# A denoising layer and a 5x5 layer on one core: cosine products on 32x32 tiles, products moved within VectorE's order, transfers written in smaller pieces

## The chip, the core and the metric

The kernel runs on one core of a Trainium2 chip, in float32 throughout. The core has TensorE (PE in the profile; its weight loads are PEld), VectorE (DVE), ScalarE (ACT), GpSimd (POOL) and SyncE (SP). POOL and SP here mostly issue transfers, which 16 DMA engines carry out. The metric is the device time of one execution in microseconds.

## The reference

The input x has 8 images of 32 channels and 128 x 128 pixels. Layer 0 normalises x in groups of two channels, finds for each pixel the 8 of 25 neighbouring offsets with the least patch distance, and gathers the 8 shifted copies into 256 channels (xb). On these it computes

```
dct    = conv1x1(xb, dct_w, groups=32)           # 8x8 blocks, one per input channel
h      = relu(depthwise3x3(conv1x1(xb, w1), w2))
h      = relu(depthwise3x3(conv1x1(h, w3), w4))
wiener = sigmoid(depthwise3x3(conv1x1(h, w5), w6))
x      = x + conv1x1(conv1x1(wiener * dct, inv_dct_w, groups=32), agg_w)
```

Layer 1 normalises the new x in the same groups, convolves every channel with one 5 x 5 kernel, and adds the result to x.

## The kernel before

**Steps.** An image is worked through in strips of 8 rows (R), 16 strips and one more step for the rows that lag behind, so 17 steps an image and 136 in all, in one loop over `s`. In each pass of the loop there are four slots, i = 3, 2, 1, 0. Slots 1 to 3 are the three blocks of a 1x1 convolution and a depthwise one, each on another strip (strip s in slot 1, s-1 in slot 2, s-2 in slot 3); slot 0 finishes the strip of slot 3: it forms the cosine transform and multiplies the sigmoid's output with it. Beside that, each slot gathers one quarter of the strip that the next pass needs: `gather_load` (L584) loads the indices as ib and the pixels as xt, `gather_select` (L610) makes one-hot rows (sel) on ScalarE, `gather_pixels` (L620) multiplies them on TensorE (pg) and copies the outcome into xb, which is stored in device memory as xbd (L640).

**The two halves of a block.** The 256 channels are two halves of 128. For one, `pointwise_t` (L680) and `depthwise_t` (L733) do both convolutions on TensorE (p at L694, pw at L751). For the other, `pointwise_v` (L659) uses TensorE (pv at L670), and `depthwise_v` (L711) does one product on ScalarE (L722) and eight multiply-adds on VectorE (L725), then the activation (L729). `depthwise_v` is a generator: the multiply-adds are written out in the slot of its block, the activation in the next slot (as `dv`), and the transfer of the two rows for the next strip in the one after it (as `kept`).

**The cosine transform.** `final_load` (L770) loads the strip's x (xr) and its 256 gathered channels (xf, one buffer) at the end of slot 0, one pass ahead of their use. `final_dct` (L796) multiplies xf with ldct on 64x64 tiles of TensorE into pc (L810), four rows at a time, each PSUM tile filled by two row groups of the array, and VectorE multiplies the blocks' output by pc in place (L818, here "the products"). `final_add` (L820) multiplies the products with lagg (pa, L831) in the next pass's slot 3; then VectorE adds xr (L839), takes statistics (L840), and four transfers store x1d (L844). ldct is made once by `mixes` (L300) from 32 small loads of dct_w on SP (dq, L308).

**PSUM.** The pool `ps_x` has five tiles of 512 columns, which pv, p, pg, pc, pa, layer 1's products and several transposes share.

**What sets the order.** The loop is written out by hand for TensorE, VectorE and ScalarE: what stands first in the code is first in the engine's order. POOL's and SP's instructions are not in that list; the framework's scheduler places their transfers, so they need not follow the code. Work for the next image (`prep`, `squares`, `costs`, `places`, `sources`) and layer 1 of the image before (`layer1`, `middle`) is cut into tasks in queues: B and D hold VectorE work with costs and due times, which `tick` spends by credit in each slot; A, P and Q hold work that is run whole at fixed places of the slot (P before `final_dct`, Q after it, A near the end). A task that yields a queue's name goes on when that queue is next run, and not before the stated number of ticks. `sources` (L399) ends in one row of some 30 transfers from POOL (xtd, L424), once an image; `costs` (L485) issues 13 (dsum, L492 and L499).

Of the kernel before, what the change touches and what calls it, by code (L numbers as in the profile page):

```python
# [20 lines left out]
R = 8  # L21
# [23 lines left out]
def bm3d_conv_preact(  # L45
# [61 lines left out]
    ldct = const.tile([P, 2, 64], F32, name="ldct")  # L107
# [96 lines left out]
    queues = {"B": deque(), "D": deque(), "A": deque(), "P": deque(), "Q": deque()}  # L204
# [95 lines left out]
    def mixes():  # L300

        dq = work.tile([P, 2, K], F32, name="dq", tag="dq", bufs=1)
        src = dct_w.rearrange("(m h c i) k a b -> m h k c (i a b)", m=2, h=2, i=K)
        for k in range(K):
            for m in range(2):
                for h in range(2):
                    p = 64 * h + 32 * (k % 2) + 8 * (k // 2)
                    nc.sync.dma_start(dq[p : p + 8, m], src[m, (h + m + 1) % 2, k])  # L308
        m8 = work.tile([P, 8], F32, name="m8", tag="m16", bufs=1)
        yield "D", 1.0, 10  # L310
        nc.vector.tensor_reduce(
            m8,
            cst[:, C_M32 : C_M32 + C].rearrange("p (a c) -> p c a", c=8),
# [3 lines left out]
        for m in range(2):  # L317
            nc.vector.tensor_tensor(
                ldct[:, m].rearrange("p (c i) -> p c i", i=K),
                m8.unsqueeze(2).to_broadcast([P, 8, K]),  # L320
                dq[:, m].unsqueeze(1).to_broadcast([P, 8, K]),
                ALU.mult,
            )
# [296 lines left out]
    def gather_pixels(b, s4, f):  # L620

        n, h = s4 // 2, s4 % 2
        if h == 0 and f == 0:
            xbs[b, n] = xbp.tile([P, 2, R, W], F32, name=f"xb_{b}_{n}", tag="xb")
        xb, xt = xbs[b, n], xts[b, s4]
        sels = [selss.pop((b, s4, f, k2)) for k2 in range(2)]
        pg = ps_x.tile([P, 2, 4, HW], F32, name=f"pg_{b}_{s4}_{f}", tag="x")
        for t in range(NT // 2):
            xa, xz = TW * t, min(TW * (t + 1), HW)
            for j in range(4):  # L630
                nc.tensor.matmul(  # L631
                    pg[C * j : C * (j + 1), :, :, xa:xz],
                    xt[: 8 * QW, f * (NT // 2) + t],
                    sels[j // 2][: 8 * QW, j % 2 * 2 : j % 2 * 2 + 2, :, xa:xz],
                    start=True,
                    stop=True,
                )
        nc.scalar.copy(xb[:, :, 4 * h : 4 * h + 4, HW * f : HW * (f + 1)], pg)
        if h == 1 and f == 1:
            nc.gpsimd.dma_start(xbd[b][:, :, R * n : R * (n + 1)], xb)  # L640
# [70 lines left out]
    def depthwise_v(i, b, n):  # L711
# [4 lines left out]
        for k, (dy, dx) in enumerate(  # L716
# [7 lines left out]
            else:  # L724
                nc.vector.scalar_tensor_tensor(  # L725
# [44 lines left out]
    def final_load(b, n):  # L770
# [15 lines left out]
        src = xbd[b].rearrange("(j m h c) g y x -> g m h j c y x", j=4, m=2, h=2)  # L786
        for m in range(2):
            for h in range(2):
                for g in range(2):
                    p = 64 * h + C * g  # L790
                    nc.gpsimd.dma_start(  # L791
                        xf[p : p + C, m, j0:j1], src[g, m, (h + m + 1) % 2, :, :, ya:yz]
                    )
        return xr, xf, j0, j1

    def final_dct(b, n, acc, xf, j0, j1):  # L796

        for r0 in range(0, R, 4):
            a, z = max(r0, j0), min(r0 + 4, j1)
            if a >= z:  # L800
                continue


            pc = [
                ps_x.tile([P, 4, W], F32, name=f"pc_{b}_{n}_{m}_{r0}", tag="x") for m in range(2)
            ]
            for h in range(2):
                for m in range(2):
                    o = 64 * ((h + m + 1) % 2)
                    nc.tensor.matmul(  # L810
                        pc[m][o : o + 64, : z - a],
                        ldct[64 * h : 64 * h + 64, m],
                        xf[64 * h : 64 * h + 64, m, a:z],
                        start=True,
                        stop=True,
                    )
            for m in range(2):
                nc.vector.tensor_mul(acc[m][:, a:z], acc[m][:, a:z], pc[m][:, : z - a])  # L818

    def final_add(b, n, acc, xr, j0, j1):  # L820
# [19 lines left out]
        nc.vector.bn_stats(stats[b][:, n], xr)  # L840
        for j in range(4):
# [6 lines left out]
    def layer1(b):  # L848
# [60 lines left out]
        for c in range(0, C, 8):  # L909
# [3 lines left out]
            yield "P", 0  # L913
# [20 lines left out]
            for e in range(2):  # L934
                y = t[2 * e]
                nc.vector.tensor_add(y, y, ps[e])
                for a, z in ((0, 62), (66, P)):
                    nc.gpsimd.dma_start(
                        out[b, c + 4 * e : c + 4 * e + 4, a:z].rearrange("c y x -> y c x"),
                        y[a:z],  # L940
# [83 lines left out]
    def turn(credit):  # L1024
# [4 lines left out]
        run("P")  # L1029
        run("Q")  # L1030
# [5 lines left out]
    with tc.manual_schedule(engines=ORDERED):  # L1036
# [3 lines left out]
        xbd[0] = dram.tile([P, 2, H, W], F32, name="xbd_0", tag="xbd")  # L1040
# [15 lines left out]
        for s in range(len(steps) + 2):  # L1056
            if s < len(steps):
# [6 lines left out]
                if n == NS - 1 and b + 1 < NB:  # L1064
                    until(lambda: b + 1 in ready, 4.0)
                    xbd[b + 1] = dram.tile([P, 2, H, W], F32, name=f"xbd_{b+1}", tag="xbd")
            for i in (3, 2, 1, 0):
# [6 lines left out]
                if live and i:  # L1074
# [3 lines left out]
                    accs[i, bi, ni] = [None, next(new_v)]  # L1078
                next(later, None)
# [6 lines left out]
                if live and not i:  # L1086
                    final_dct(bi, ni, accs[3, bi, ni], xf, j0, j1)

# [14 lines left out]
                next(dv, None)  # L1103
# [3 lines left out]
                next(dt, None)  # L1107
                kept, dv, dt = dv, new_v, new_t
                if live and not i:
                    later = end(bi, ni, xr, j0, j1)  # L1110
                if not i and 0 <= s - 1 < len(steps):
                    fins[s - 1] = final_load(*steps[s - 1])
# [66 lines left out]
```

## Time and profile before

| | |
|---|---|
| median of 3 runs | 6535.1 us (6530.16 to 6537.6) |
| the profiled execution | 6526.97 us |
| its span | 6525.2 us |
| granted TensorE clock, mean | 0.979 of full speed |
| PE, DVE, ACT, POOL busy | 95%, 90%, 77%, 47% of the span |
| transfers | 886.21 MB in 544960 packets, 136 GB/s |
| first and last pc (L810) | 287.9 and 6459 us |

A group of the profile names the line, the engine, the operation, and the tiles as out<-in, with how often it occurs, its busy time, the mean of one, and the idle time of its engine just before it with what ended that idle time. A line of waits reads: the engine and the tile that waited, what it waited for, the sum of the waits in us, how many, and the longest. In a line of the timeline stand start and length in us, and instructions of one kind in a row are put together, their number behind x. A float32 matmul of the code is two records.

### The profile page before, as it was taken

To read this page: it belongs to the slowest core of one execution; us is meant where nothing else is said; L and a number is where in the kernel's file an instruction comes from. 1 tells how busy PE (TensorE), PEld (TensorE's weight loads), DVE (VectorE), ACT (ScalarE), POOL (GpSimd) and SP (SyncE) were. 2 spreads that over 40 slices of the span, in tenths; PEclk is the share of its full clock that TensorE was granted. 3 is DMA by queue.
4 is the path that set the end of the run, shared out by engine and by line. 5 is a ranking of instruction groups with operands and counts; after the bars stand their busy time and mean duration, and the time that the engine had idled before them with its cause. 6 is when DMAs were issued, how large, how long until landed. Compare 5 with 4: busy or idle time off the path is not lost.

```text
span 6525.2 us, 234180 instructions
## 1 busy us (share of the span) xinstructions
PE 6180.3 (95%) x102306; PEld 3262.3 (50%) x102306; DVE 5856.5 (90%) x8828; ACT 5051.0 (77%) x6698; POOL 3077.3 (47%) x5015
## 2 busy tenths in 40 slices
PE   5799999999999999999999999999999999999997
PEld 1445445544555546454555544544545454465553
DVE  7899988999889998899998999899998999988776
ACT  5787769778787877877778787887869787787772
POOL 8345436444364444643446534454345644344334
PEclk7899999999999999999999999999999999999998
DMA  4555555565555655655546556565555665455553
GB/s 85 125 135 144 123 124 146 145 143 135 133 145 139 142 147 127 150 140 135 141 129 157 140 131 151 127 150 137 139 134 138 150 147 133 118 149 147 137 135 79
DMA packets 544960, 886.21 MB, mean 136 GB/s; under 512 B 248880, under 2 KB 312944, under 8 KB 543936
## 3 DMA queue, kind: packets, MB, share of 16 engines
q0 software_dynamic: 383648, 611.87, 37.4%
q1 hardware_dynamic: 157776, 258.11, 16.4%
q8 instruction: 805, 13.19, 0.9%
q10 hardware_dynamic: 2512, 1.25, 0.1%
q14 instruction: 219, 1.79, 0.1%
HBM read 420.60 MB, written 216.49 MB: 98 GB/s over the span
## 4 chain that ended last, share of the span: by engine, by line
PE 50%; DVE 32%; ACT 5%; POOL 5%; DMA 4%; issue 4%; SPq 0%; ACTq 0%; DVEq 0%; POOLq 0%
DVE acc L725 21%; PE pw L751 16%; PE pv L670 12%; PE p L694 11%; PE pg L631 4%; DVE idx L537 3%; POOL xtd L424 3%; PE pc L810 2%; DVE df L444 2%; DVE acc L818 1%; PE p L924 1%; DVE mx L536 1%; PE pd L459 1%; DMA t<-t 1%; ACT sel L616 1%
## 5 line engine op out<-in xcount | busy, mean ns | idle before, releaser
L725 DVE SCALAR_TENSOR_TENSOR acc<-tv,dwv,acc 128x1024 f32<-128x1024 f32 (+3 forms) x3264 | 4031.6, 1237 | 156.3 <-ACT acc L722 52.0
L751 PE MATMUL pw<-t,dwd 96*32 96x254 f32 (+7 forms) x31680 | 2118.1, 419 | 23.0 <-DMA t<-t 10.1
L751 PEld LDWEIGHTS pw<-t,dwd 96*32 96x32 f32 (+1 forms) x31680 | 1105.7, 110 | 826.8 <-issue 369.3
L616 ACT ACTIVATE sel<-ib,nplace 128x1024 f32<-128x1024 uint8 x1024 | 1170.8, 1143 | 62.0 <-DMA ib<-idxd 62.0
L617 ACT ACTIVATE sel<-sel 128x1024 f32<-128x1024 f32 x1024 | 1086.0, 1061 | 32.5
L670 PE MATMUL pv<-acc,lw 128*32 128x512 f32 x8448 | 959.8, 590 | 54.4 <-DVE acc L818 47.8
L694 PE MATMUL p<-acc,lw 128*32 128x256 f32 x16768 | 974.3, 379 | 2.2 <-issue 2.2
L602 POOL DMA_DIRECT2D ib<-idxd x512 | 292.0, 570 | 1207.3 <-ACT sel L616 1078.1
L791 POOL DMA_DIRECT2D xf<-xbd x1088 | 651.0, 632 | 279.9 <-PE pc L810 180.6
L694 PEld LDWEIGHTS p<-acc,lw 128*32 128x32 f32 x16768 | 570.7, 111 | 393.6 <-issue 67.4
L729 ACT ACTIVATE acc<-acc 128x1024 f32<-128x1024 f32 (+3 forms) x408 | 417.1, 1022 | 390.2 <-DVE acc L725 389.8
L678 ACT COPY tv<-pv 128x512 f32<-128x512 f32 (+2 forms) x784 | 435.9, 579 | 338.5 <-PE pv L670 334.1
L631 PE MATMUL pg<-sel,xt 120*32 120x88 f32 (+1 forms) x24576 | 611.7, 244 | 64.8 <-ACT sel L617 56.1
L631 PEld LDWEIGHTS pg<-sel,xt 120*32 120x32 f32 x24576 | 559.5, 111 | 219.2 <-ACT sel L617 74.4
L670 PEld LDWEIGHTS pv<-acc,lw 128*32 128x32 f32 x8448 | 290.2, 110 | 532.3 <-issue 409.7
L764 ACT ACTIVATE acc<-pw 128x512 f32<-128x512 f32 (+2 forms) x808 | 436.6, 572 | 133.4 <-PE pw L751 131.8
L444 DVE TENSOR_TENSOR df<-xn 128x786 f32<-128x786 f32 (+2 forms) x576 | 530.4, 972 | 2.2 <-PE pd L459 1.9
L701 ACT COPY t<-p 128x512 f32<-128x512 f32 x800 | 421.7, 571 | 115.4 <-PE p L694 115.4
L452 ACT ACTIVATE df<-df 128x786 f32<-128x786 f32 (+2 forms) x576 | 458.9, 859 | 50.0 <-DVE df L444 48.6
L722 ACT ACTIVATE acc<-tv,dwv 128x1024 f32<-128x1024 f32 (+3 forms) x408 | 455.1, 1115 | 42.3 <-PE pa L831 24.8
L670 PE MATMUL pv<-xb,lw 128*32 128x512 f32 x4096 | 470.8, 596 | 0.0
L694 PE MATMUL p<-xb,lw 128*32 128x256 f32 x8192 | 469.9, 380 | 0.0
(155 smaller groups left out, 5893.0 us busy)
## 6 DMA issues: line engine op xcount, KB each, us to landing
ib<-idxd POOLq DMA_DIRECT2D x512, 256.0 KB, 4.0
xbd<-xb POOLq DMA_DIRECT2D x128, 1024.0 KB, 6.0
xf<-xbd POOLq DMA_DIRECT2D x960, 128.0 KB, 6.8
t<-t SPq DMA_DIRECT2D x792, 128.0 KB
t<-t SPq DMA_DIRECT2D x384, 256.0 KB
tv<-tv SPq DMA_DIRECT2D x384, 130.0 KB
xt<-xtd POOLq DMA_DIRECT2D x240, 180.0 KB, 4.0
xtd<-xl POOLq DMA_DIRECT2D x192, 96.0 KB, 3.3
```

What stands on the lines that cost most here:

```text
L444: nc.vector.tensor_sub(df[:, :, ca:cz], xn[:, r0 : r0 + SR, ca:cz], xn[:, r0 + dy : r0 + dy + SR, ca + dx : cz + dx],)
L452: nc.scalar.activation(df[:, :, ca:cz], df[:, :, ca:cz], AF.Square)
L616: nc.scalar.activation(sel, ib, AF.Square, bias=nplace)
L617: nc.scalar.activation(sel, sel, AF.Relu, scale=-1.0, bias=1.0)
L631: nc.tensor.matmul(pg[C * j : C * (j + 1), :, :, xa:xz], xt[: 8 * QW, f * (NT // 2) + t], sels[j // 2][: 8 * QW, j % 2 * 2 : j % 2 * 2 + 2 ...
L670: nc.tensor.matmul(ps[C * j : C * (j + 1), :hr], lhsT[:, g, P + C * j : P + C * (j + 1)], src(g)[:, h : h + hr], start=g == 0, stop=g == 1,)
L694: nc.tensor.matmul(ps[C * r : C * (r + 1), e, :nb], lhsT[:, g, s], rows[:, r : r + 4 * nb - 3 : 4], start=g == 0, stop=g == 1,)
L722: nc.scalar.activation(acc, rows, AF.Copy, scale=tap)
L725: nc.vector.scalar_tensor_tensor(acc, rows, tap, acc, op0=ALU.mult, op1=ALU.add)
L751: nc.tensor.matmul(pt[u][C * j : C * (j + 1), ka:kz, :nb, xa:xz], dwd[0:hi, i - 1, u, j, dx + 1], t[0:hi, j, ka:kz, :nb, xa + dx : xz + dx ...
L764: nc.scalar.activation(rows[:, u : u + 2 * nh[u] - 1 : 2, :nb], pt[u][:, : nh[u], :nb], funcs[i - 1])
L791: nc.gpsimd.dma_start(xf[p : p + C, m, j0:j1], src[g, m, (h + m + 1) % 2, :, :, ya:yz])
```

## The change

The cosine transform goes from 64x64 to 32x32 tiles. ldct holds four 32 x 32 blocks per partition group rather than two of 64 columns, made from 64 small loads rather than 32. In `final_dct`, s counts four parts (two halves of the channels times two groups of four rows), each with its own PSUM tile, and q four row groups of the array; part s takes from row group q to column group (q + s) % 4, so that each PSUM tile is filled by all four row groups. All 16 matmuls of a strip now come before the first product.

xbd is laid out by channel. A strip is stored in two times four transfers, after each four rows, rather than in one. xf is loaded part by part, up to seven transfers in place of eight: the first part at the end of slot 0, the second at the end of the next pass's slot 3, the last two at the end of its slot 2.

In the first block, `depthwise_v` stops after six of its eight multiply-adds; the last two are written out in slot 0 behind `final_dct`, and its activation moves to the next pass's slot 3.

The four x1d transfers of `final_add` and the four output transfers of `layer1` are written some way behind the VectorE instructions that make their data. Layer 1's matmuls get a queue of their own, L, which is run in place of `final_dct` where a slot has none.

```diff
--- before.py
+++ after.py
@@ -104,7 +104,7 @@
     lw5 = const.tile([P, 2, CK], F32, name="lw5")
 
 
-    ldct = const.tile([P, 2, 64], F32, name="ldct")
+    ldct = const.tile([P, 4, C], F32, name="ldct")
     lagg = const.tile([P, 2, C], F32, name="lagg")
 
 
@@ -201,7 +201,7 @@
 
 
 
-    queues = {"B": deque(), "D": deque(), "A": deque(), "P": deque(), "Q": deque()}
+    queues = {"B": deque(), "D": deque(), "A": deque(), "P": deque(), "L": deque(), "Q": deque()}
 
     PAIR = 1.95
     pairs = [0]
@@ -299,26 +299,26 @@
 
     def mixes():
 
-        dq = work.tile([P, 2, K], F32, name="dq", tag="dq", bufs=1)
-        src = dct_w.rearrange("(m h c i) k a b -> m h k c (i a b)", m=2, h=2, i=K)
-        for k in range(K):
-            for m in range(2):
-                for h in range(2):
-                    p = 64 * h + 32 * (k % 2) + 8 * (k // 2)
-                    nc.sync.dma_start(dq[p : p + 8, m], src[m, (h + m + 1) % 2, k])
-        m8 = work.tile([P, 8], F32, name="m8", tag="m16", bufs=1)
+        dq = work.tile([P, 4, K], F32, name="dq", tag="dq", bufs=1)
+        src = dct_w.rearrange("(m q c i) k a b -> m q c k (i a b)", m=2, q=4, i=K)
+        for s in range(4):
+            for q in range(4):
+                for c in range(4):
+                    p = C * q + K * c
+                    nc.sync.dma_start(dq[p : p + K, s], src[s // 2, (q + s) % 4, c])
+        m4 = work.tile([P, 4], F32, name="m4", tag="m16", bufs=1)
         yield "D", 1.0, 10
         nc.vector.tensor_reduce(
-            m8,
-            cst[:, C_M32 : C_M32 + C].rearrange("p (a c) -> p c a", c=8),
+            m4,
+            cst[:, C_M32 : C_M32 + C].rearrange("p (a c) -> p a c", a=4),
             axis=mybir.AxisListType.X,
             op=ALU.add,
         )
-        for m in range(2):
+        for s in range(4):
             nc.vector.tensor_tensor(
-                ldct[:, m].rearrange("p (c i) -> p c i", i=K),
-                m8.unsqueeze(2).to_broadcast([P, 8, K]),
-                dq[:, m].unsqueeze(1).to_broadcast([P, 8, K]),
+                ldct[:, s].rearrange("p (c i) -> p c i", i=K),
+                m4.unsqueeze(2).to_broadcast([P, 4, K]),
+                dq[:, s].unsqueeze(1).to_broadcast([P, 4, K]),
                 ALU.mult,
             )
 
@@ -636,8 +636,14 @@
                     stop=True,
                 )
         nc.scalar.copy(xb[:, :, 4 * h : 4 * h + 4, HW * f : HW * (f + 1)], pg)
-        if h == 1 and f == 1:
-            nc.gpsimd.dma_start(xbd[b][:, :, R * n : R * (n + 1)], xb)
+        if f == 1:
+            for j in range(4):
+                nc.gpsimd.dma_start(
+                    xbd[b].rearrange("(c j g) y x -> j c g y x", j=4, g=2)[
+                        j, :, :, 4 * s4 : 4 * s4 + 4
+                    ],
+                    xb[C * j : C * (j + 1), :, 4 * h : 4 * h + 4],
+                )
 
 
 
@@ -722,6 +728,8 @@
                 nc.scalar.activation(acc, rows, AF.Copy, scale=tap)
                 yield out_
             else:
+                if i == 1 and k == 7:
+                    yield
                 nc.vector.scalar_tensor_tensor(
                     acc, rows, tap, acc, op0=ALU.mult, op1=ALU.add
                 )
@@ -783,39 +791,41 @@
             )
 
         xf = xbp.tile([P, 2, R, W], F32, name=f"xf_{b}_{n}", tag="xf", bufs=1)
-        src = xbd[b].rearrange("(j m h c) g y x -> g m h j c y x", j=4, m=2, h=2)
-        for m in range(2):
-            for h in range(2):
-                for g in range(2):
-                    p = 64 * h + C * g
+        yield xr, xf, j0, j1
+        src = xbd[b].rearrange("(m p) y x -> m p y x", m=2)
+        for s in range(4):
+            if s:
+                yield
+            m, r0 = s // 2, s % 2 * 4
+            a, z = max(r0, j0), min(r0 + 4, j1)
+            for pa, pz, at in ((0, P - C * s, C * s), (P - C * s, P, 0)):
+                if a < z and pa < pz:
                     nc.gpsimd.dma_start(
-                        xf[p : p + C, m, j0:j1], src[g, m, (h + m + 1) % 2, :, :, ya:yz]
+                        xf[pa:pz, m, a:z],
+                        src[m, at : at + pz - pa, R * n - 3 + a : R * n - 3 + z],
                     )
-        return xr, xf, j0, j1
+        yield
 
     def final_dct(b, n, acc, xf, j0, j1):
 
-        for r0 in range(0, R, 4):
-            a, z = max(r0, j0), min(r0 + 4, j1)
-            if a >= z:
-                continue
-
-
-            pc = [
-                ps_x.tile([P, 4, W], F32, name=f"pc_{b}_{n}_{m}_{r0}", tag="x") for m in range(2)
-            ]
-            for h in range(2):
-                for m in range(2):
-                    o = 64 * ((h + m + 1) % 2)
-                    nc.tensor.matmul(
-                        pc[m][o : o + 64, : z - a],
-                        ldct[64 * h : 64 * h + 64, m],
-                        xf[64 * h : 64 * h + 64, m, a:z],
-                        start=True,
-                        stop=True,
-                    )
-            for m in range(2):
-                nc.vector.tensor_mul(acc[m][:, a:z], acc[m][:, a:z], pc[m][:, : z - a])
+        parts = [(s, max(s % 2 * 4, j0), min(s % 2 * 4 + 4, j1)) for s in range(4)]
+        parts = [(s, a, z) for s, a, z in parts if a < z]
+        pc = {
+            s: ps_x.tile([P, 4, W], F32, name=f"pc_{b}_{n}_{s}", tag="x") for s, a, z in parts
+        }
+        for q in range(4):
+            for s, a, z in parts:
+                o = C * ((q + s) % 4)
+                nc.tensor.matmul(
+                    pc[s][o : o + C, : z - a],
+                    ldct[C * q : C * (q + 1), s],
+                    xf[C * q : C * (q + 1), s // 2, a:z],
+                    start=True,
+                    stop=True,
+                )
+        for s, a, z in parts:
+            m = s // 2
+            nc.vector.tensor_mul(acc[m][:, a:z], acc[m][:, a:z], pc[s][:, : z - a])
 
     def final_add(b, n, acc, xr, j0, j1):
 
@@ -838,6 +848,7 @@
         yield
         nc.vector.tensor_add(xr, xr, pa)
         nc.vector.bn_stats(stats[b][:, n], xr)
+        yield
         for j in range(4):
             ra = ya + 2 * j if whole else ya
             xa = 0 if whole else C * j
@@ -910,7 +921,7 @@
             if c == 0 or not last:
                 yield "D", 2.0, 1 if last else 3
                 normalise(c)
-            yield "P", 0
+            yield "L", 0
             ps = [
                 ps_x.tile([P, 4, W], F32, name=f"p5_{b}_{c}_{e}", tag="x") for e in range(2)
             ]
@@ -932,12 +943,13 @@
             if last and c + 8 < C:
                 normalise(c + 8)
             for e in range(2):
-                y = t[2 * e]
-                nc.vector.tensor_add(y, y, ps[e])
+                nc.vector.tensor_add(t[2 * e], t[2 * e], ps[e])
+            yield "A", 0, 1
+            for e in range(2):
                 for a, z in ((0, 62), (66, P)):
                     nc.gpsimd.dma_start(
                         out[b, c + 4 * e : c + 4 * e + 4, a:z].rearrange("c y x -> y c x"),
-                        y[a:z],
+                        t[2 * e][a:z],
                     )
             if c + 8 < C and not last:
                 yield "A", 0, 1
@@ -1027,6 +1039,7 @@
         run("B")
         run("A")
         run("P")
+        run("L")
         run("Q")
 
     def until(cond, credit):
@@ -1037,7 +1050,7 @@
         push(prep(0))
         push(weights())
         push(mixes())
-        xbd[0] = dram.tile([P, 2, H, W], F32, name="xbd_0", tag="xbd")
+        xbd[0] = dram.tile([CK, H, W], F32, name="xbd_0", tag="xbd")
         for i in range(3):
             nc.gpsimd.memset(tb[i][0:64, 0], 0.0)
         for u in range(7):
@@ -1076,6 +1089,8 @@
                     pointwise_v(i, bi, ni, lws[i - 1], src)
                     new_v, new_t = depthwise_v(i, bi, ni), depthwise_t(i, bi, ni)
                     accs[i, bi, ni] = [None, next(new_v)]
+                if i == 3:
+                    next(kept, None)
                 next(later, None)
                 if live and not i:
                     if ni == 0:
@@ -1085,6 +1100,10 @@
                 run("P")
                 if live and not i:
                     final_dct(bi, ni, accs[3, bi, ni], xf, j0, j1)
+                else:
+                    run("L")
+                if not i:
+                    next(dv, None)
 
                 run("Q")
                 if s < len(steps):
@@ -1100,16 +1119,22 @@
                     unit(gather_pixels, u)
                 next(dt, None)
                 run("A")
-                next(dv, None)
+                if i:
+                    next(dv, None)
                 if s < len(steps):
                     unit(gather_select, u + 1, (1,))
                     u += 1
                 next(dt, None)
+                next(later, None)
                 kept, dv, dt = dv, new_v, new_t
                 if live and not i:
                     later = end(bi, ni, xr, j0, j1)
                 if not i and 0 <= s - 1 < len(steps):
-                    fins[s - 1] = final_load(*steps[s - 1])
+                    loads = final_load(*steps[s - 1])
+                    fins[s - 1] = next(loads)
+                if 0 <= s - (1 if not i else 2) < len(steps):
+                    for _ in range({0: 1, 3: 1, 2: 2, 1: 0}[i]):
+                        next(loads)
         next(kept, None)
         for _ in later:
             pass
...
```

The hunk left out changes the shape of xbd[b + 1] like that of xbd[0].

More of the change, by code (lines that the diff above doesn't have):

```diff
@@ L1065, in bm3d_conv_preact @@
                     until(lambda: b + 1 in ready, 4.0)
[L1066 removed]
+                    xbd[b + 1] = dram.tile([CK, H, W], F32, name=f"xbd_{b+1}", tag="xbd")
             for i in (3, 2, 1, 0):
```

## The prediction

> **What bounds the kernel now.** First the busy times and the 40 slices of the page.
>
> ```profile
> PE 6180.3 (95%) x102306; PEld 3262.3 (50%) x102306; DVE 5856.5 (90%) x8828; ACT 5051.0 (77%) x6698; POOL 3077.3 (47%) x5015
> PE   5799999999999999999999999999999999999997
> DVE  7899988999889998899998999899998999988776
> ```
>
> PE is full from the third slice on, DVE nearly so. Then the stretch from the first cosine product (pc, L810) to the last, and two single steps in it, each from one step's pc to the next.
>
> ```profile
> 287.90:6459.00 6171.10, 5972.12 (x100058) 3171.29 (x100054) 5600.56 (x8145) 4869.65 (x6449) 2867.30 (x4719) 0.99 0.55 138
> 2836.20:2885.30 49.10, 49.10 (x820) 24.37 (x820) 46.61 (x81) 41.20 (x53) 19.85 (x34) 1.00 0.61 152
> 3032.00:3080.60 48.60, 45.40 (x778) 23.10 (x774) 47.09 (x80) 37.63 (x50) 13.11 (x24) 1.00 0.49 121
> ```
>
> The columns are window, length, then busy time of PE, PEld, DVE, ACT and POOL. Over the stretch PE is idle for 199 us of 6171. In the step at 2836 PE has no gap at all. In the step at 3032 PE is idle for 3.2 us, while DVE misses only 1.5 us over 80 instructions, about 20 ns each, which is no more than the seam between two instructions: that step is DVE's. So two engines take turns as the bound, step by step. Whatever PE saves counts only in PE's steps.
>
> Last the waits between these two.
>
> ```profile
> PE pv L670 <- DVE acc L818: 47.8, 28, 3.6
> DVE xr L839 <- PE pa L831: 261.2, 69, 9.8
> ```
>
> PE waits 47.8 us for the products (L818), which hold four of the five PSUM tiles that pv needs; DVE waits 261 us for pa.
>
> **Part 1: the cosine product on 32x32 tiles.**
>
> ```profile
> 3308.16 1.95 PE L810 MATMUL pc<-xf,ldct 64*64 64x512 f32 x16
> 3310.04 5.37 PE L751 MATMUL pw<-t,dwd 96*32 96x256 f32 x96
> 3315.22 3.62 PE L670 MATMUL pv<-acc,lw 128*32 128x512 f32 x32
> 3318.66 1.04 PE L831 MATMUL pa<-acc,lagg 128*32 128x256 f32 x16
> 3322.97 1.14 PE L631 MATMUL pg<-sel,xt 120*32 120x88 f32 x48
> 3323.92 3.63 PE L670 MATMUL pv<-acc,lw 128*32 128x512 f32 x32
> ```
>
> A matmul of the code is two records (8 in the code, x16 here). From start to next start pc takes 1.88 us per whole step: 16 records of 512 columns on four tiles, so 0.47 us for four at once. pv, also four tiles, takes 3.44/32 x 4 = 0.43 us. The new form has 16 matmuls, 32 records of 512 columns, for 16 tiles. No row shows more than four tiles at once, so I bound it. If all 16 overlap, it is two rounds of 0.43, 0.86 us; the shortest spacing in these rows, 0.95/48 = 20 ns in pg, asks 0.63 us for 32 records and doesn't bind. If only four overlap, it is 32 x 0.43/4 = 3.44 us. I take 1.0 us, near the low end: in today's pc two row groups write different partitions of the same bank, and the four still run nearly as pv's four do (0.47 against 0.43), so row groups don't hold each other up.
>
> The rule "TensorEngine Tiling (Array Packing)", Restrictions and Gotchas, speaks against this: different row tiles cannot access the same PSUM bank simultaneously, and here all four row groups write all four banks. If that forced row groups one after the other, today's pc would be 8 x 0.43 = 3.4 us rather than 1.88, so the trace disagrees for two row groups; with the rule the new pc would be 3.44 us. "TensorE: Matmul & The Clock Gate", Part 3, has 16 tiles at 10.6 times one tile; by that it would be about 32 x 0.43/10.6 = 1.3 us, an estimate.
>
> PE saves 0.88 us a step. The columns of all pc records make 128 whole steps, so 113 us. What arrives: for each of the 135 stretches from pc to pc I took the larger of PE's busy time and DVE's (plus 22 ns per instruction for the seams). The sum is 6120 us now and 6054 us with PE 0.88 lower: 66 us. The rest is lost in the 55 stretches where DVE is already longer.
>
> **Part 2: products (L818) after six of the eight multiply-adds.** DVE's work is unchanged: the same four products of 679 ns and eight multiply-adds of 1284 ns (L725), two of which now come behind the products. So the products come up to 2.6 us earlier, and their PSUM tiles come free. DVE waits only 10.5 us in all for pc (L818 <- PE pc), and in the steps I read the first product starts 5 to 10 us after pc, so products can mostly move up. That frees PE's 47.8 us of waits, mean 1.7 us, and puts 2.6 us of work ahead of DVE's wait for pa. Bounds: 0 to 70 us gained (47.8 and 4.4 and some of pa's); half of the PE wait in a kernel whose DVE is full elsewhere, so I take 25 us. The activation of the first block's output moves one slot back, behind pv's copies; ACT now waits 389.8 us for L725 at L729, so it is late anyway. Nothing.
>
> **Part 3: transfers.** Per whole step xbd goes from one store to 8, xf from 8 loads to 7. Issues in all: 128 stores (0.716 us each) become 1024, at the 0.632 us of an xf issue of the same 128 KB; 1088 loads become 920. That is 1024 x 0.632 - 92 - 168 x 0.632 = +449 us on POOL, 3077 to about 3530 (54%). POOL idles in waits: 1078 us for ACT's sel alone, which covers 3.5 us a step. It doesn't cover the 7 steps in which 30 xtd transfers stand in one row:
>
> ```profile
> 3476.30 1.25 POOL L791 DMA_DIRECT2D xf<-xbd  x2
> 3478.73 24.64 POOL L424 DMA_DIRECT2D xtd<-xl  x30 [1.19 <-DMA xl<-xs]
> ...
> 3507.03 0.75 POOL L640 DMA_DIRECT2D xbd<-xb  x1
> 3507.65 3.49 POOL L791 DMA_DIRECT2D xf<-xbd  x6
> ```
>
> ```profile
> 3519.13 1.09 PE L810 MATMUL pc<-xf,ldct 64*64 64x512 f32 x8
> 3522.11 2.46 PE L810 MATMUL pc<-xf,ldct 64*64 64x512 f32 x8 [1.89 <-ACT t L701]
> ```
>
> The xf loads end their issue at 3511.1, land by about 3519 (up to 8.8 us here), and pc starts at 3519.1: no slack. Four stores instead of one ahead of them cost 1.9 us there; 7 x 1.5 = 10 us lost. The x1d and out stores that now come later take waits out of POOL's queue (308 us x1d <- DVE xr, 87 us out_dram <- DVE xy); what waits behind them is ib, two units ahead, so I count nothing. The L queue takes layer 1's matmuls out of the slot of pc: the same PE work elsewhere, nothing.
>
> **Part 4: the start.**
>
> ```profile
> 23.40 23.00 SPq L308 DMA_DIRECT2D dq<-in_L_conv_dct_w_dram  x32
> 53.55 0.40 DVE L318 TENSOR_TENSOR ldct<-m,dq 128x64 f32<-128x64 f32 x2
> ```
>
> 64 dq loads at 0.72 us end at 69.4 on SP rather than 46.4, and land some 2 us later. DVE wants them at 53.5, so DVE waits about 18 us, with the squares of the first image (L444) queued behind. Part is made good, since DVE idles 6 us at 73 anyway and POOL's 22.5 us of xtd fall in this time: 0 to 18, I take 12.
>
> **Sum** against the profiled execution: 6527.0 us around a span of 6525.2; -66 - 25 + 10 + 12 = -69, 6458. The median of the runs shown is 8.1 us above that execution, so 6466 by the median.
>
> **Rivals.** *A, xf too late.* In the 7 steps with the xtd row, POOL runs behind PE; the last four xf loads are now written two slots before their use, and if dsum's 13 transfers (7.8 us, L492 and L499) and x1d's four come ahead, they land some 12 us after PE gets to pc. 7 x 12 = 84 us instead of 10: 6540. For it: the missing slack above. Against it: POOL's order isn't that of the code (xr was issued 24 us early), and xf may be put ahead. It decides from about 9 us of lateness a time on.
> *B, the tiles don't overlap beyond four (the slower one).* Place: L810, every step. Price: 3.5 - 1.88 = 1.62 us; the same sum of larger busy times gives +147, and with the other terms 6535 + 147 - 25 + 22 = 6679. It decides from pc at about 1.9 us a step. For it: no row has 16 tiles. Against it: two row groups at once in today's pc.
> *C, DVE takes it all.* If the products now wait for pc and DVE's seams leave no room, 66 becomes 20 and 25 becomes 0: 6535 - 20 + 22 = 6537. Against it: PE is without a gap in steps like that at 2836.
> *D, more than forecast.* All 113 us and 50 of waits: 6535 - 163 + 12 = 6384.
>
> **Numbers.** Forecast 0.50 (6420 to 6512), A 0.17 (6512 to 6570), B 0.13 (6640 to 6720), C 0.12 (6505 to 6545), D 0.08 (6370 to 6420). Range 6405 to 6570: it leaves out B and most of D. A difference of 0.2% (13 us) is about what a measurement of this kernel can tell from none. Faster: the forecast, D, half of C and a sixth of A, 0.67. Same: most of the rest of C and a third of A, 0.11. Slower: B and half of A, 0.22.
>
> **What would show it.** Part 1: pc at about 1.0 us a step, x32 records; at 1.9 or more it is wrong. Part 2: PE's wait for L818 under 20 us, DVE's wait for pc not over 40. Part 3: POOL near 3530 us; PE waits at L810 for DMA xf, if over 40 us, speak for A. Part 4: a DVE wait for dq near 54 us. DVE busy stays at 5856. What would make it wrong: transfers in POOL's queue that hold back ib, and with it sel and pg, in ordinary steps too.

## The result and the profile after

The changed kernel takes 6561.2 us (median of 5 runs, 6556.4 to 6570.2); the kernel before, timed in the same series, 6533.1 us (5 runs). The ratio is 1.0059, 95% interval 1.0048 to 1.0070: slower by 0.6%, where 1% faster was forecast. The profiled execution took 6562.4 us around a span of 6560.6, at a mean granted clock of 0.970 (0.979 before).

The page's busy times, two of its slices, and its row for the stores of xbd (issues, size, median us to landing):

```profile
PE 6115.5 (93%) x104418; PEld 3340.8 (51%) x104418; DVE 5841.6 (89%) x8830; ACT 5050.2 (77%) x6698; POOL 3394.7 (52%) x5743
PE   5798999999999999999999999999999999999997
DVE  7798988989989999899998999889999899988786
xbd<-xb POOLq DMA_DIRECT2D x1024, 128.0 KB, 3.7
```

PE has 65 us less to do than before, DVE 15 us less, and the kernel is 35 us longer: the time lies in gaps. The waits of PE and DVE say which:

```profile
PE pc L819 <- DMA xf<-xbd: 61.6, 7, 10.7
PE pv L676 <- DVE acc L828: 25.0, 8, 3.5
PE pd L459 <- ACT sm L470: 29.0, 7, 4.3
DVE xr L849 <- PE pa L841: 149.4, 48, 6.0
DVE acc L828 <- PE pc L819: 112.7, 41, 12.6
```

The first line is new: seven times, once for each image but one, pc waits about 9 us for its loads (0.8 us, once, before). The second was 47.8 us before, the third 2.7 us once, the fourth 261.2, the fifth 10.5. PE's wait of pi for oc, not shown, goes from 67.2 to 87.6 us. So three things moved: the loads of xf, the order of products and pa, and something in the index work (pd and sm, pi and oc).

One step without such a wait, PE's timeline:

```profile
3322.43 5.34 PE L759 MATMUL pw<-t,dwd 96*32 96x512 f32 x48
3327.70 1.15 PE L819 MATMUL pc<-xf,ldct 32*32 32x512 f32 x32
3328.77 5.38 PE L759 MATMUL pw<-t,dwd 96*32 96x256 f32 x96
```

From start to next start pc takes 1.07 us for 32 records, against 1.88 before. The part of the change that gave it its name works as forecast.

Now the step after the row of xtd transfers, first POOL's issues, then PE:

```profile
3496.56 1.60 POOL L803 DMA_DIRECT2D xf<-xbd  x3
3498.62 24.64 POOL L424 DMA_DIRECT2D xtd<-xl  x30 [0.47 <-issue]
...
3526.94 2.21 POOL L641 DMA_DIRECT2D xbd<-xb  x4
3529.12 0.59 POOL L602 DMA_DIRECT2D ib<-idxd  x1
3529.69 0.69 POOL L492 DMA_DIRECT2D dsum<-sq  x1
3530.36 3.61 POOL L499 DMA_DIRECT2D dsum<-sq  x6
...
3539.68 2.33 POOL L855 DMA_DIRECT2D x1d<-xr  x4
...
3545.28 1.57 POOL L803 DMA_DIRECT2D xf<-xbd  x3
3547.23 0.52 POOL L803 DMA_DIRECT2D xf<-xbd  x1 [0.38 <-DMA ib<-idxd]
```

```profile
3540.05 1.05 PE L819 MATMUL pc<-xf,ldct 32*32 32x512 f32 x4
3549.55 3.92 PE L819 MATMUL pc<-xf,ldct 32*32 32x512 f32 x28 [8.45 <-DMA xf<-xbd]
```

Three of the seven loads are issued ahead of the row. The other four, now written later in the code, come behind dsum's 13 and x1d's four, the last at 3547.2; PE is at pc at 3540 and gets on at 3549.5. That is what rival A describes.

### The profile page after: what moved, and what is told of

Read it like the earlier page. It is cut to its first block, busy times and chain, and to the rows that moved or that the text cites. A ratio compares the mean times of both kernels' runs of the same rounds, so it can differ in the third digit from the quotient of the medians.

```text
span 6560.6 us, 239359 instructions
## 1 busy us (share of the span) xinstructions
PE 6115.5 (93%) x104418; PEld 3340.8 (51%) x104418; DVE 5841.6 (89%) x8830; ACT 5050.2 (77%) x6698; POOL 3394.7 (52%) x5743
## 4 chain that ended last, share of the span: by engine, by line
PE 41%; DVE 30%; ACT 11%; POOL 7%; DMA 5%; issue 5%; ACTq 0%; SPq 0%; POOLq 0%; DVEq 0%
DVE acc L733 19%; PE pw L759 15%; PE pv L676 10%; PE p L700 9%; DVE idx L537 3%; PE pg L631 3%; ACT sel L616 2%; POOL xtd L424 2%; ACT df L452 2%; DVE df L444 2%; PE p L935 2%; PE pc L819 1%; DVE mx L536 1%; DMA ib<-idxd 1%; DVE acc L828 1%
## 5 line engine op out<-in xcount | busy, mean ns | idle before, releaser
L759 PEld LDWEIGHTS pw<-t,dwd 96*32 96x32 f32 (+1 forms) x31680 | 1131.3, 110 | 800.1 <-issue 371.0
L700 PE MATMUL p<-acc,lw 128*32 128x256 f32 x16768 | 995.2, 383 | 0.6 <-issue 0.6
L700 PEld LDWEIGHTS p<-acc,lw 128*32 128x32 f32 x16768 | 617.6, 112 | 361.4 <-issue 73.2
L641 POOL DMA_DIRECT2D xbd<-xb x1024 | 552.2, 546 | 269.4 <-ACT xb L638 174.9
L631 PE MATMUL pg<-sel,xt 120*32 120x88 f32 (+1 forms) x24576 | 618.6, 244 | 62.2 <-ACT sel L617 53.3
L803 POOL DMA_DIRECT2D xf<-xbd x920 | 482.6, 530 | 367.5 <-PE pc L819 318.1
L602 POOL DMA_DIRECT2D ib<-idxd x512 | 306.7, 599 | 679.4 <-ACT sel L616 645.0
L676 PEld LDWEIGHTS pv<-acc,lw 128*32 128x32 f32 x8448 | 304.0, 111 | 526.6 <-issue 385.6
L855 POOL DMA_DIRECT2D x1d<-xr x544 | 274.9, 511 | 473.0 <-DVE xr L849 445.8
```

What stands on the lines that cost most here:

```text
L631: nc.tensor.matmul(pg[C * j : C * (j + 1), :, :, xa:xz], xt[: 8 * QW, f * (NT // 2) + t], sels[j // 2][: 8 * QW, j % 2 * 2 : j % 2 * 2 + 2 ...
L641: nc.gpsimd.dma_start(xbd[b].rearrange("(c j g) y x -> j c g y x", j=4, g=2)[j, :, :, 4 * s4 : 4 * s4 + 4], xb[C * j : C * (j + 1), :, 4 * ...
L676: nc.tensor.matmul(ps[C * j : C * (j + 1), :hr], lhsT[:, g, P + C * j : P + C * (j + 1)], src(g)[:, h : h + hr], start=g == 0, stop=g == 1,)
L700: nc.tensor.matmul(ps[C * r : C * (r + 1), e, :nb], lhsT[:, g, s], rows[:, r : r + 4 * nb - 3 : 4], start=g == 0, stop=g == 1,)
L759: nc.tensor.matmul(pt[u][C * j : C * (j + 1), ka:kz, :nb, xa:xz], dwd[0:hi, i - 1, u, j, dx + 1], t[0:hi, j, ka:kz, :nb, xa + dx : xz + dx ...
L803: nc.gpsimd.dma_start(xf[pa:pz, m, a:z], src[m, at : at + pz - pa, R * n - 3 + a : R * n - 3 + z],)
```

## Experiments

Each ratio is to the kernel before, run on the same chip. The experiments ran on three chips; where two of them are compared, it is taken that such a ratio carries over from one chip to another. The expectations speak of four theories. L: the last four xf loads come too late in seven steps. S: POOL now has too many transfers everywhere. Y: layer 1's work falls into steps that are full. Z: the fifth step grows because of the tiles and the four PSUM tiles that pc holds.

**The loads.** All seven loads written at the end of slot 0 again, where the kernel before has its eight.

```diff
                     fins[s - 1] = next(loads)
-                if 0 <= s - (1 if not i else 2) < len(steps):
-                    for _ in range({0: 1, 3: 1, 2: 2, 1: 0}[i]):
-                        next(loads)
+                    for _ in loads:
+                        pass
```

> The changed kernel, but all seven xf loads are written at the end of slot 0, as before the change. Theory L (xf comes too late): PE's 61.6 us of waits at pc for DMA xf fall under 15, the second step of an image loses its extra 3.6 us, and the time falls by 30 to 45 us, to about 6520. Theory S (POOL has too many transfers, wherever they are written): the stores still stand in front of the loads, the wait stays over 40 us, and the time stays within 10 us of 6561.

Measured 0.9973 (0.9960 to 0.9985), 6506.9 us. There is no wait of pc for xf any more, and DVE's for pc shrinks:

```profile
PE pv L676 <- DVE acc L828: 26.0, 8, 3.5
```

```profile
DVE xr L849 <- PE pa L841: 177.3, 50, 7.1
DVE acc L828 <- PE pc L819: 45.3, 36, 2.8
```

0.0086 of 6530 us is 56 us, with the two intervals put together 45 to 67. That is more than the 30 to 45 that theory L had, near the 61.6 us of the wait, and enough to turn the sign. PE's wait of pd for sm stays at 29.0 us.

**Layer 1.** Two of the smaller edits undone, each alone in the changed kernel: its matmuls run from queue P again, and its output transfers written right behind the additions.

```diff
-            yield "L", 0
+            yield "P", 0
```

> The changed kernel, but layer 1's matmuls go into queue P again (run before pc in slot 0 as well) rather than into L. Theory Y (layer 1's work now falls into the steps that are full already): the fifth step of an image loses most of its extra 12.9 us, offset by some 4 us in the fourth, so the time falls by 30 to 60 us. Theory L or S: no change beyond 10 us.

```diff
                 nc.vector.tensor_add(t[2 * e], t[2 * e], ps[e])
-            yield "A", 0, 1
-            for e in range(2):
                 for a, z in ((0, 62), (66, P)):
```

> The changed kernel, but layer 1's four output transfers are written right behind the additions again, so that each group of channels needs one tick less. Theory Y, if it is the tick that shifts the work: the fifth step of an image loses most of its extra 12.9 us and the time falls by 30 to 60 us. If it is the queue L that shifts it: no change beyond 10 us, and the run with the queue put back shows the gain.

Measured 1.0038 (1.0024 to 1.0052) and 1.0035 (1.0026 to 1.0045). Both keep the wait of pc for xf (62.6 and 62.4 us). Each is some 0.2% better than the change (14 and 16 us by the ratios); the first interval just touches the change's, the second just misses it. Theory Y had 30 to 60 us for the one of the two that shifts the work; neither gives that.

**The tiles alone.** The kernel before with the 32x32 tiles and what they need: the layout of xbd by channel with four stores a strip, the seven loads at the end of slot 0, and the queue L. Products, x1d's and layer 1's transfers are as before.

```diff
+            for j in range(4):
+                nc.gpsimd.dma_start(
+                    xbd[b].rearrange("(c j g) y x -> j c g y x", j=4, g=2)[
+                        j, :, :, R * n : R * (n + 1)
+                    ],
+                    xb[C * j : C * (j + 1)],
+                )
...
-            yield "P", 0
+            yield "L", 0
```

> The kernel before with the 32x32 tiles alone: pc as changed, xbd laid out by channel and stored after each strip in four transfers of eight rows, all seven xf loads at the end of slot 0, multiply-adds, x1d and output transfers as before. Queue L is kept, since pc now holds four PSUM tiles at once. If the tiles' gain is as worked out (PE 0.8 us less a step, of which a little over half arrives) and the loss lies in the rest of the change: 6535 less 50 to 70 us, about 6475. If the gain is lost to DVE or to the four PSUM tiles that pc now takes at once: 6520 to 6560.

Measured 0.9953 (0.9935 to 0.9970), 6493.3 us: 31 us gained where the prediction has 66, and a time between the two that were expected. The page and two waits of PE:

```profile
PE 6104.3 (94%) x104418; PEld 3293.5 (51%) x104418; DVE 5853.5 (90%) x8830; ACT 5044.5 (78%) x6698; POOL 3101.9 (48%) x5231
```

```profile
PE pv L676 <- DVE acc L826: 66.4, 33, 4.5
PE pd L459 <- ACT sm L470: 28.3, 7, 4.3
```

By the groups of the profile pc's own busy time falls by 102 us (281.8 to 179.6). Other matmuls come out 26 us longer, so PE's sum falls by 76. The mean granted clock is lower, 0.976 against 0.979: by the trace's record of the clock PE works at half of it for 218 us, before for 188, and half of the difference, 15 us, would be the clock's part in the 26 (an estimate). Of the 76, 43 us are new idle time, chiefly in these two lines (18.6 and 25.6 us more than before), and 33 us leave the span.

**The queue alone.** The second line of these can't come from the tiles if it is there without them. So the kernel before with queue L and nothing else.

```diff
-            yield "P", 0
+            yield "L", 0
...
         run("P")
+        run("L")
...
                     final_dct(bi, ni, accs[3, bi, ni], xf, j0, j1)
+                else:
+                    run("L")
```

> The kernel before, with queue L alone: 64x64 tiles, old transfers, old order of products; only layer 1's matmuls are kept out of the slot of pc. Theory Y (a group of them then lands in the slot in which the next image's index transposes, pi, also stand, in the fifth step of six images): that step grows by 9 to 13 us and the fourth shrinks by 4 to 5, so the time rises by 25 to 50 us, ratio 1.004 to 1.008. Rival Z (the fifth step grows because of the tiles or the four PSUM tiles that pc takes): no change beyond 0.2%.

Measured 1.0015 (1.0005 to 1.0024): 10 us, 3 to 16, lost by the order alone. PE's waits:

```profile
PE pv L670 <- DVE acc L818: 46.4, 23, 3.6
PE pd L459 <- ACT sm L470: 29.1, 7, 4.3
```

The wait of pd for sm is all there, without a tile changed; the time is less than the 25 to 50 us that theory Y had. Where the wait lies shows when each image's 17 steps are taken from the first pc record of one to that of the next, and the mean made over six images (us, worked out from the trace; step 5 begins with pc of strip 4):

| step | before | after | loads early | tiles alone | L alone |
|---|---|---|---|---|---|
| 2 | 59.01 | 62.61 | 54.38 | 56.10 | 58.84 |
| 4 | 49.59 | 45.31 | 44.30 | 44.64 | 46.69 |
| 5 | 48.40 | 61.34 | 61.38 | 60.06 | 57.46 |
| 8 | 48.11 | 46.05 | 46.28 | 45.35 | 45.39 |
| 10 | 44.20 | 47.18 | 46.72 | 43.75 | 44.28 |
| all 17 | 786.1 | 793.2 | 783.9 | 782.5 | 789.2 |

Step 2 is the one behind the xtd row: the late loads cost 8.2 us there (62.61 against 54.38), and seven of them make 58. Step 5 is 9 to 13 us longer in each of the four kernels; 9 of these are there without the tiles, which leaves theory Z 3 or 4 at most. The steps around it become shorter, so that with the queue alone all 17 grow by 3.1 us only. With the matmuls back in P (the second experiment) step 5 is still 7.7 us longer, so the queue is not alone in this, and without the added yield (the third) it is 60.6 us, as long as in the change: that tick is not what lengthens it. The changed kernel's PE and DVE in one such step:

```profile
3711.08 0.41 PE L569 MATMUL pi<-cst,oc 128*128 128x128 f32 x2 [4.24 <-DVE oc L560]
3711.42 6.18 PE L935 MATMUL p<-xm,band 64*64 64x512 f32 x40
3717.53 3.66 PE L700 MATMUL p<-acc,lw 128*32 128x256 f32 x64
...
3730.50 1.55 PE L459 MATMUL pd<-df,neg 128*32 128x396 f32 x8 [4.28 <-ACT sm L470]
3731.83 5.58 PE L700 MATMUL p<-acc,lw 128*32 128x256 f32 x64
```

```profile
3717.65 1.28 DVE L946 TENSOR_TENSOR xy<-xy,p 128x512 f32<-128x512 f32 x2 [3.16 <-PE p L935]
```

A group of layer 1 (p, L935) now falls beside the index work of the next image (oc, pi, pd, sm). PE waits for DVE, DVE for PE, and PE for ACT, in one step that had room for one of the two.

The granted clock adds to it. Here is step 5 of one image, first before the change and then after it: window, length, the busy time of PE, PEld, DVE, ACT and POOL, then the clock, the DMA share and GB/s. The third line is PE alone in the stretch right behind the wait for sm.

```profile
3678.33:3725.14 46.81, 46.31 (x783) 24.23 (x775) 43.15 (x58) 37.94 (x51) 27.50 (x40) 1.00 0.58 143
3694.97:3757.08 62.11, 53.59 (x839) 27.23 (x835) 52.79 (x60) 42.85 (x57) 35.26 (x55) 0.92 0.59 145
3730.50:3737.23 6.73, 6.73 (x73) 0.61 0.38 97
```

In that stretch the clock is 0.61, and p's 64 records take 5.58 us, where 64 of the same shape took 3.66 at 3717. So the wait of 4.28 us cost more than its length. In the six steps of the table the clock is 0.89 to 0.94 with the change; before it is 1.00 in five of them and 0.97 in one.

**Another place for that group.** On the first experiment, layer 1's next group falls due a tick later.

```diff
-                yield "D", 2.0, 1 if last else 3
+                yield "D", 2.0, 1 if last else 4
```

> The changed kernel with its loads at the end of slot 0, and layer 1's next group due four ticks after its loads rather than three, so that no group stands in the slot of pi in the fifth step. Theory Y: the fifth step falls from 61 to about 49 us, the time by 30 to 60 us against the kernel with early loads, to 6450 to 6480, ratio to before 0.988 to 0.993. Rival Z: 6500 to 6515, ratio 0.996 to 0.998.

Measured 1.0036 (1.0022 to 1.0050), 0.6% worse than without it. Theory Y had 0.988 to 0.993. Step 5 falls from 61.4 to 45.6 us, as the theory wants. But against the first experiment step 8 grows by 9.7, step 11 by 6.5, step 6 by 4.4 and step 4 by 4.0:

```profile
PE pi L569 <- DVE oc L560: 108.3, 22, 20.2
PE pt L525 <- issue: 74.5, 19, 4.8
```

The first line was 87.9 us in the first experiment, and the second has no counterpart of more than 4 us in the other kernels. The collision exists, but delaying all groups moves it to other steps. The part of the theory that said it could be had back by the due time falls.

**The products.** On the first experiment, the products and activation of the first block back where they were, behind all eight multiply-adds.

```diff
-                if i == 1 and k == 7:
-                    yield
...
-                if i == 3:
-                    next(kept, None)
...
-                if not i:
-                    next(dv, None)
...
-                if i:
-                    next(dv, None)
+                next(dv, None)
```

> The changed kernel with its loads at the end of slot 0 and the products behind all eight multiply-adds again. If moving the products was worth something (25 us by the prediction): 15 to 35 us slower than with early loads alone, ratio to before 1.000 to 1.003, PE's wait at pv for L828 back at 50 us or more. If it was worth nothing: within 8 us, ratio 0.996 to 0.998.

Measured 0.9970 (0.9960 to 0.9979) against 0.9973: nothing, within 0.16% either way. The waits do move:

```profile
PE pv L676 <- DVE acc L826: 67.8, 46, 4.5
```

```profile
DVE xr L847 <- PE pa L839: 237.2, 61, 7.2
```

Without the edit PE waits 42 us more for the products and DVE 60 us more for pa. These sums do not turn into time. By the pages PE's idle time is only 13 us less with the edit (386.9 us against 400.1), so most of the 42 is waited elsewhere; and its busy time is 13 us more (6113.3 against 6100.5) at a lower granted clock (0.974 against 0.978). Step by step, the edit takes 1.9 us from step 9 (47.6 to 45.7) and adds 2.4 to step 10 (44.4 to 46.7).

**The stores.** On the first experiment, a strip stored in four transfers of eight rows rather than eight of four.

```diff
-        if f == 1:
+        if h == 1 and f == 1:
...
-                        j, :, :, 4 * s4 : 4 * s4 + 4
+                        j, :, :, R * n : R * (n + 1)
...
-                    xb[C * j : C * (j + 1), :, 4 * h : 4 * h + 4],
+                    xb[C * j : C * (j + 1)],
```

> The changed kernel with its loads at the end of slot 0, and each strip stored in four transfers of eight rows after its last quarter rather than two times four of four rows: 4 issues a step less, about 270 us less of POOL's busy time. If POOL's number of transfers costs time (theory S): 10 to 25 us faster than with early loads alone, ratio 0.993 to 0.996. If it is hidden: within 8 us, ratio 0.996 to 0.9985.

Measured 0.9980 (0.9969 to 0.9991) against 0.9973: 512 transfers fewer give no gain. Theory S is out, as far as it rests on the stores.

**The row of xtd transfers.** If a row of 30 transfers decides the sign, it can be cut: after every second column the task ends its turn in queue P. First in the changed kernel, then with the loads early and layer 1's transfers back, in the tiles alone, and in the kernel before.

```diff
         for j in range(QW):
+            if j % 2:
+                yield "P", 0
```

> The changed kernel as it is, late loads and all, but the row of 30 xtd transfers is cut into eight pieces, one a slot. Theory L says that the late loads cost time only because POOL runs behind PE after that row: PE's 61.6 us of waits at pc for DMA xf fall under 15, and the time falls by 40 to 60 us, to 6500 to 6520 (ratio to before 0.995 to 0.999). If the loads are late for where they are written, row or no row: wait over 40, time within 15 us of the changed kernel's.

> The changed kernel with the loads at the end of slot 0, layer 1's output transfers right behind the additions, and the xtd row cut into eight pieces. Theory L: once the loads are early, the row costs only what it costs the kernel before (7 waits of sel for ib), 10 to 25 us, and the stores some 13 us: 6465 to 6490, ratio 0.991 to 0.995.

> The 32x32 tiles alone on the kernel before, with the xtd row cut into eight pieces. Against the tiles alone (ratio 0.9953) it loses the waits of sel for ib behind the row: ratio 0.990 to 0.994. It should be the fastest of all if products, x1d and output transfers moved are worth nothing.

> The kernel before with the xtd row cut into eight pieces and nothing else, to tell what the cut is worth by itself. ACT's 62 us of waits of sel for ib fall by half or more; the time falls by 5 to 25 us, ratio 0.996 to 0.999. If the cut alone gives 40 us or more, the gain of the changed kernel with the cut is not that of the late loads.

| | as it was | row cut |
|---|---|---|
| before | 1 | 0.9938 (0.9925 to 0.9952) |
| the change | 1.0059 (1.0048 to 1.0070) | 0.9925 (0.9912 to 0.9939) |
| loads early, layer 1's transfers back | not run | 0.9910 (0.9895 to 0.9926) |
| tiles alone | 0.9953 (0.9935 to 0.9970) | 0.9904 (0.9889 to 0.9919) |

POOL's issues in the changed kernel with the row cut:

```profile
3468.02 3.28 POOL L426 DMA_DIRECT2D xtd<-xl  x4
3471.29 0.56 POOL L593 DMA_DIRECT2D xt<-xtd  x1
3471.84 0.58 POOL L604 DMA_DIRECT2D ib<-idxd  x1
3473.32 2.19 POOL L643 DMA_DIRECT2D xbd<-xb  x4 [0.91 <-ACT xb L640]
3475.51 2.10 POOL L805 DMA_DIRECT2D xf<-xbd  x4
3478.14 3.28 POOL L426 DMA_DIRECT2D xtd<-xl  x4 [0.54 <-DMA xbd<-xb]
```

Four xtd transfers at a time now stand between the others, and xf isn't held up: no wait of pc for xf is left. The kernel before gains 0.62% too, 40 us (32 to 49) where 5 to 25 were expected; its row held back the index loads. This line of ScalarE's waits is its own, and is gone when the row is cut:

```profile
ACT sel L616 <- DMA ib<-idxd: 62.0, 14, 10.3
```

Step 2 of the kernel before falls from 59.0 to 53.3 us, and seven such steps make 40. So the changed kernel's gain, 87 us where 40 to 60 were expected, is not that of the late loads alone: some 40 are what the row costs without them, and the 47 that are left fit the first experiment's 56, given that each has some 11 to 14 us either way.

With the row cut, all of the change together is worth 0.13%, which the intervals don't separate from nothing. The tiles alone are worth 0.34%, and there the intervals are apart. That version, 6469.7 us, has the lowest ratio of all, 1% below the kernel before; the one with loads early and layer 1's transfers back, 0.9910, is too near for the intervals to separate.

## Why the prediction was wrong

**The step that failed is in Part 3:** "Four stores instead of one ahead of them cost 1.9 us there; 7 x 1.5 = 10 us lost." The stores were not what mattered. Four of the seven loads are written later, and in seven steps they are issued behind dsum and x1d: 56 us (45 to 67) by the first experiment. The prediction named this as rival A, with the place, the seven times and 84 us, and gave it 0.17. Its argument against it, that the scheduler may put xf ahead, failed: in the step shown they are behind. A had 12 us a time; the trace has 8.8. That the 6561 lies in the band given to A (6512 to 6570) is partly luck: A's sum had 84 us for the loads and kept all of Parts 1 and 2, while the loads cost 56 and Parts 1 and 2 gave less.

**Part 1: the mechanism right, the yield too high.** pc takes 1.07 us rather than 1.0, so the row groups hardly hold each other up, and rival B is out. PE's busy time falls with it, but 31 us arrive, not 66. Of the missing 35, some 10 are the queue L, which the prediction counted at nothing. That leaves about 41, worked out from two runs and good to some 13 us, if the queue costs the same beside the tiles. The estimate took the larger of PE's and DVE's busy time per step and so left out waits that arise when PE comes sooner: the wait of pv for the products grew by 18.6 us. It also took PE's other work to stay as fast as it was, which the lower granted clock (0.976) did not allow: some 15 us by the estimate above. Whether these two make up the rest was not tested.

The Trainium skill, "TensorEngine Tiling (Array Packing)", Restrictions and Gotchas, says that row tiles can't access one PSUM bank at the same time. All four row groups write all four banks here, 32 records in 1.07 us, where a round of pv's four tiles (128x32) takes 0.43 us, so that one row group after the other would be 3.44: the measurement disagrees with the rule for this shape. "TensorE: Matmul & The Clock Gate", Part 3, with 10.6 times one tile, gave an estimate of 1.3 us; the 1.07 measured is less.

**Part 2: 25 us are 0.** The forecast waits did fall (PE's for the products to 25.0, not quite under 20), and DVE's for pc passed 40 even with the loads early (45.3). Undone, the edit costs no time. The step that failed is "half of the PE wait in a kernel whose DVE is full elsewhere": none of it came, to within 10 us.

**"The same PE work elsewhere, nothing".** Queue L costs 10 us by itself, because work of the same length put into another step meets the index work there. The later output transfers, also counted at nothing, cost about 16 us by the third experiment (6 to 25). Their place was thought to matter only to POOL's queue. But the added yield also puts off layer 1's next group by a tick. How the 16 us come about stays open: the three us that step 10 is longer are not it, since they are there without the yield too (46.9 us in the third experiment) and go when the products are put back (44.4). The execution that the third experiment's trace shows is only 4 us shorter than the change's (6558.8 against 6562.4 us), so it doesn't show where the 16 lie.

**Part 4: 12 us are about 2.** The 64 loads went out at 0.375 us each, not 0.72, and were done before DVE came to them:

```profile
23.66 24.01 SPq L308 DMA_DIRECT2D dq<-in_L_conv_dct_w_dram  x64
```

```profile
54.19 0.19 DVE L318 TENSOR_TENSOR ldct<-m,dq 128x32 f32<-128x32 f32 x1 [0.18 <-issue]
```

The first pc stands at 290.05 us, 2.2 later than before. POOL came to 3395 us rather than 3530 for the same reason: the price of a transfer was taken from another shape.

**The sum.** From the kernel before to tiles alone -31 us, from there to the first experiment +13 (this difference has an interval of about 14 either way), from there to the change +56: +38, which is 0.0059 of 6533. These are differences of measured ratios in a row, so that they add up is no proof of the parts; each part stands on its own run.

**What stays open.** What keeps the tiles alone from more than about 41 us: the new waits, the clock, or something else. What layer 1 would cost beside the tiles with its matmuls in P and its transfers at once, both together: that was not tried. And what the change without its late loads, and with nothing else undone, gains over a kernel whose xtd row is cut; with layer 1's transfers back as well it is 0.28% (0.9910 against 0.9938), and the two intervals meet at their ends.

## What to carry to other kernels

A load that is split so that its parts are written nearer to their use gives up slack, and it must be held against the longest row of transfers on its queue, not the usual one. Work that an engine does "elsewhere" has a price set by the step it lands in: compare the kernels step by step, since sums of busy time and of waits hide one step that grows by 13 us while its neighbours shrink, and look at the granted clock in that step too. And before a row of transfers is worked around, try cutting it: one added yield gained 0.6% here by itself, and 1.3% with the change in place, part of which is the late loads' loss made good.

## What the runs showed of the hardware

Sixteen 32x32 tiles run nearly side by side: 1.07 us for 32 records of 512 columns, where two rounds at pv's 0.43 would be 0.86. The price of issuing a transfer depends on its shape: POOL took 546 ns for a store of four rows of the new xbd, 547 for one of eight rows (tiles alone) and 716 for the old one of the whole strip, 530 rather than 632 ns for an xf load, 0.82 us for xtd; SP took 375 ns for one of the 64 dq loads and 720 for one of the 32. The cut row and the whole row cost POOL the same per transfer (3.28 us for four, 24.64 for 30); only what stands behind them differs. Behind a wait of 4.28 us PE's granted clock was 0.61 for 6.7 us, and 64 records that took 3.66 us elsewhere in the step took 5.58.
